# A new order for the pieces of two interleaved layers: where transposes, scores and roundings stand in each step's queue

## The chip, the cores and the metric

The kernel runs on one core of a Trainium2 chip. A core has a matrix engine (TensorE, "PE" in the profile, with its weight loads as "PEld"), a vector engine (VectorE, "DVE"), an activation engine (ScalarE, "ACT"), a general engine (GpSimd, "POOL") and a queue engine that issues transfers ("SP"). Each engine works through its own list of instructions in order; semaphores make one engine wait for another. The metric is the device time of one execution in microseconds (us).

## The reference

Eight layers are applied to `x` (16 batches x 128 tokens x 256 columns, float32), each as `x = x + tanh(gate) * layer(layernorm(x))`. Four are attention-like, four are feed-forward. The change touches mainly the part of the program in which three of them are computed together: the grouped-query attention of layer pair 1, its feed-forward layer with rounded weights and activations, and the decayed running sum of layer pair 2.

```python
# attention of pair 1: 16 query heads of 16 columns, 4 key heads, context as keys and values
Q = (query @ Wq).reshape(b, q_len, G, Hpg, dh) / math.sqrt(dh)
scores = einsum('bqghd,bkgd->bghqk', Q, K) + m * rel          # ALiBi slopes
out = einsum('bghqk,bkgd->bqghd', softmax(scores), V) @ Wo
# feed-forward of pair 1
def act_quant(x):
    scale = 127.0 / clip(max(abs(x), axis=-1, keepdims=True), EPS)
    return clip(round(x * scale), -128.0, 127.0) / scale
def weight_quant(w):
    scale = 1.0 / clip(mean(abs(w)), EPS)
    return clip(round(w * scale), -1.0, 1.0) / scale
bitlinear = lambda x, w: einsum('bsd,hd->bsh', act_quant(x), weight_quant(w))
y = bitlinear(silu(bitlinear(x, w1)) * bitlinear(x, w3), w2)   # 256 -> 704 -> 256
# layer of pair 2: r = decay * r + k*v along the tokens, out = q * r   (k = v = context)
```

## The kernel before

`stage_l1x` (from line 991) is the joint pipeline. Its main loop (line 1140) counts steps `n` from -4 to 22. In step `n` the attention of batch `n` is in the middle of its way: its scores and exponentials are made (`weigh`, two halves of two key heads each), while batch `n-1` is multiplied with its values (`mix`) and normalised, batch `n-2` is turned and projected (`turn_o`, `output`), and batch `n+4` gets the expert outputs of the layer before and its layernorm statistics (`collect`, `stats`). Queries are made for two batches at once, one half of the heads in an even step and the other half in an odd one.

`following` (line 1172) supplies the layers that follow. Here two batches, a pair `q`, go through together, over six steps. Batches `2q` and `2q+1` leave the attention in step `2q+3`; then come, in steps `2q+3` to `2q+8`: statistics (`stats`), normalisation and the largest magnitude (`normal`, `largest`), rounding (`rounded`), a transpose (`turn`), the two up-projections per batch with SiLU (`up`), rounding of the hidden row (`hidden`), its six transposes (`turn_hidden`), the down-projection (`down`), the squares and decayed sums of the context (`scanned`), and the layer of pair 2 (`retain_normal`, `retain`). The dictionary `order` (line 1413) says in which step after `2q+3` and at which of four places of that step a piece is issued; `then(m, place)` issues what stands there. A second list, `early` (line 1264), rounds the three weight matrices in steps 0 to 5: `total` sums magnitudes (VectorE), `size` adds them over the partitions (a small matmul), `rounded_weight` scales and rounds (ScalarE), `integers` clips (VectorE). From step 6 on the weights of the next stage are fetched by six transfers on POOL's queue.

For PE, VectorE and ScalarE the order of instructions is written out by hand (`manual_schedule`, line 996): each of these engines executes exactly in the order in which the Python code issues. POOL and SP are ordered by the compiler framework.

Two pools of PSUM hold what PE writes. `pss` has two buffers of two banks each (tag "s"): scores `s`, the up-projection `fu` and the hidden transposes `fh` go there in turn. `pst` has four buffers of one bank each (tag "a"), for everything else. PE can't write a buffer before its previous contents have been read. So for instance the scores of a step wait until ScalarE has copied `fh`, and the second half of an up-projection waits until VectorE has multiplied the first.

Names in the profile: `to` turn_o, `av` mix, `tx` turn_x, `tq` queries, `y` output, `ta` normalise, `fx` turn, `fh` turn_hidden, `fu` up, `fy` down, `fr` retain, `ts` size, `pt` the exponentials, `avs`, `oT`, `xT`, `qa` the copies out of PSUM.

Of the kernel before, what the change touches and what calls it, by code (L numbers as in the profile page):

```python
# [14 lines left out]
ALU = mybir.AluOpType  # L15
AX = mybir.AxisListType
# [39 lines left out]
def passage(ctx: ExitStack, tc: tile.TileContext, a: dict, out: bass.AP, inv, flag):  # L56
# [934 lines left out]
    def stage_l1x(wq, wo, ka, vbuf, collect, work, follow):  # L991


        with tc.tile_pool(name="l1", bufs=1) as l1, tc.tile_pool(name="l1w", bufs=2) as wk_, tc.tile_pool(
# [104 lines left out]
            def normalise(b):  # L1099
# [6 lines left out]
                sums_seen(0, rc.rearrange("p j g -> p (j g)"))  # L1106
                os_[b] = wk_.tile([P, 4, 4, 16], F32, name="o")
                nc.vector.tensor_tensor(os_[b].rearrange("p g j d -> p j g d"), t[:, :, :, 0:16], bc(rc, 3, 16), ALU.mult)

# [29 lines left out]
            begun, then = follow(pss, pst)  # L1139
            for n in range(-4, B + 7 + e):  # L1140
                p, odd = divmod(n, 2)
                fill()
                when(turn_o, n - e - 2)
                then(n - e, 0)
# [4 lines left out]
                when(mix, n - e - 1)  # L1149
                then(n - e, 1)  # L1150
                if search:
                    when(top, n, 1)
                if odd:
                    when(queries, p + 1, 1, n=B // 2)
                else:
                    when(turn_x, p + 1, n=B // 2)
                when(normal, n + 4)
                if n < 0:
                    fill()
                then(n - e, 2)  # L1160
                when(output, n - e - 2)
                when(weigh, n - e, 0)
                if not odd:
                    when(queries, p + 1, 0, n=B // 2)
                when(normalise, n - e - 1)
                when(weigh, n - e, 1)
                if n >= 0:
                    begun(n)
                then(n - e, 3)


    def following(sh, dcol):
# [6 lines left out]
        def follow(pss, pst):  # L1179
# [74 lines left out]
            def integers(i):  # L1254
# [10 lines left out]
                0: [layout],  # L1265
                1: [lambda: total(0), lambda: total(1)],
                2: [lambda: total(2), size, lambda: rounded_weight(0)],
                3: [lambda: integers(0), lambda: rounded_weight(1)],
                4: [lambda: integers(1), lambda: rounded_weight(2)],
                5: [lambda: integers(2)],  # L1270
            }

            def begun(n):
                if n == 0:
                    assert not work
                for f in early.get(n, ()):
                    f()
                if n == 6:
                    l2we.append(moe2_weights())
                if n >= 6 and l2we[0][1]:  # L1280
                    l2we[0][1].pop(0)()
# [56 lines left out]
            def up(q, i):  # L1338
# [21 lines left out]
                hm = v[f"hm{q % 2}"]  # L1360
                nc.vector.tensor_reduce(
# [68 lines left out]
            def then(m, place):  # L1430
                for (d, at), fs in order.items():
                    q, odd = divmod(m - 3 - d, 2)
                    if at == place and not odd and 0 <= q < B // 2:
                        for f in fs:
                            f(q)

            return begun, then

        return follow

# [624 lines left out]
```

## Time and profile before

| | |
|---|---|
| time before, median of 3 runs | 1077.6 us (1077.56 to 1077.85) |
| the profiled execution | 1077.04 us, span 1075.3 us |
| mean granted clock of PE | 0.904 |
| busy over the span: PE, DVE, ACT, POOL | 84%, 56%, 42%, 32% |
| joint pipeline, step 0 (first scores) to the last instruction of `retain` | 353.2 to 583.8 us |
| steps 0 to 15 (with scores) end | 537.3 us |
| 451.1 to 501.5 us, four full steps: PE, DVE, ACT busy | 43.8, 39.4, 34.1 of 50.4 us |

A line of the timeline gives the start, the busy time of the merged run of instructions, the engine, the line of the code, the operation, output and inputs, the number of instructions, and in brackets how long the engine had been idle and who ended that. A line of windows gives, for a stretch, its length and then the busy time of PE, PEld, DVE, ACT and POOL with the number of instructions, the share of the full clock that was granted to PE, and the load of the transfers. The granted clock is 1.00 or 0.50 at any moment.

### The profile page before, as it was taken

To read this page: it belongs to the slowest core of one execution; us is meant where nothing else is said; L and a number is where in the kernel's file an instruction comes from. 1 tells how busy PE (TensorE), PEld (TensorE's weight loads), DVE (VectorE), ACT (ScalarE), POOL (GpSimd) and SP (SyncE) were. 2 spreads that over 40 slices of the span, in tenths; PEclk is the share of its full clock that TensorE was granted. 3 is DMA by queue.
4 is the path that set the end of the run, shared out by engine and by line. 5 is a ranking of instruction groups with operands and counts; after the bars stand their busy time and mean duration, and the time that the engine had idled before them with its cause. 6 is when DMAs were issued, how large, how long until landed. Compare 5 with 4: busy or idle time off the path is not lost. (4 is left out here: it accounts for less than half of the span.)

```text
span 1075.3 us, 14892 instructions
## 1 busy us (share of the span) xinstructions
PE 904.1 (84%) x5212; PEld 602.5 (56%) x5212; DVE 607.5 (56%) x1537; ACT 456.8 (42%) x707; POOL 342.3 (32%) x389
## 2 busy tenths in 40 slices
PE   3899978899999888888864858998169999998797
PEld 1444456677778444455443747887145555555564
DVE  5988966322225656787788586454345555534442
ACT  1211024223322446666762242454257777882111
POOL 5766322543115324211111046550443342201000
PEclk9999979999999978999986557899579999997999
DMA  9100070233341109800000202352488887530000
GB/s 305 41 1 1 0 220 21 63 104 109 69 143 50 39 20 144 78 1 1 1 1 1 78 1 88 109 145 82 142 247 235 220 222 195 164 79 1 20 30 32
DMA packets 71401, 94.12 MB, mean 88 GB/s; under 512 B 9271, under 2 KB 63127, under 8 KB 69015
## 3 DMA queue, kind: packets, MB, share of 16 engines
q1 hardware_dynamic: 56952, 67.21, 21.1%
q0 software_dynamic: 14080, 23.78, 11.4%
q10 hardware_dynamic: 288, 2.10, 0.5%
q8 instruction: 45, 0.74, 0.3%
q14 instruction: 36, 0.29, 0.1%
HBM read 57.06 MB, written 33.55 MB: 84 GB/s over the span
## 5 line engine op out<-in xcount | busy, mean ns | idle before, releaser
L1667 ACT ACTIVATE pt<-s 128x1024 f32<-128x1024 f32 x128 | 126.4, 1024 | 32.5 <-PE s L1660 29.8
L709 POOL DMA_INDIRECT yc<-ys,pos x64 | 62.4, 975 | 125.0 <-DVE x L729 49.2
L297 PE MATMUL y<-kv,toep 128*128 128x512 f32 x192 | 86.6, 602 | 1.6 <-DVE toep L237 1.6
L1660 PE MATMUL s<-qa,ka 64*128 64x256 f32 x512 | 64.3, 332 | 8.3 <-ACT pt L1667 7.5
L1676 PE MATMUL av<-pt,v 128*32 128x256 f32 x1024 | 69.4, 389 | 0.1
L289 POOL TENSOR_TENSOR kv<-ctxT 128x1024 f32<-128x1024 f32 x32 | 60.2, 1900 | 28.3 <-PE y L297 28.3
L1660 PEld LDWEIGHTS s<-qa,ka 64*128 64x128 f32 x512 | 38.6, 188 | 46.9 <-issue 23.2
L1687 DVE COPY avs<-av 128x256 f32<-128x256 f32 x64 | 27.1, 423 | 65.5 <-PE av L1676 48.5
L297 PEld LDWEIGHTS y<-kv,toep 128*128 128x128 f32 x192 | 35.6, 192 | 43.7 <-issue 40.3
L616 PE MATMUL ub<-L0we,xbT 128*128 x160 | 50.8, 460 | 2.6 <-ACT xbT L607 2.6
L593 POOL DMA_INDIRECT xb<-xs,who x40 | 38.2, 954 | 43.3 <-PE tb L605 33.2
L913 PE MATMUL yb<-L2we,hT 88*128 (+1 forms) x224 | 41.7, 315 | 9.6 <-DVE hT L737 3.9
L848 POOL DMA_INDIRECT xb<-xs,who x40 | 38.1, 953 | 31.7 <-PE tb L860 20.9
L302 DVE TENSOR_TENSOR pr<-y,qT 128x1024 f32<-128x1024 f32 x32 | 39.0, 1222 | 12.1 <-PE y L297 9.4
L1567 POOL TENSOR_TENSOR hl<-f,hl 128x512 fp32r<-128x512 f32 x16 | 20.5, 1282 | 79.5 <-ACT hl L1566 79.5
L477 PE MATMUL up<-L0s,xT 128*128 128x352 f32 x128 | 43.0, 482 | 0.0
L913 PEld LDWEIGHTS yb<-L2we,hT 88*128 88x128 f32 x224 | 33.6, 205 | 16.5 <-DVE hT L737 9.0
L1086 PE MATMUL s<-qa,ka 18*128 18x512 f32 x128 | 37.4, 660 | 4.9 <-ACT follow L1380 4.9
L305 DVE TENSOR_REDUCE oT<-pr 128x128 f32<-128x1024 f32 x32 | 38.9, 1219 | 1.0
L1676 PEld LDWEIGHTS av<-pt,v 128*32 128x32 f32 x1024 | 26.9, 110 | 20.4 <-issue 0.7
L642 PE MATMUL yb<-L0we,hTb 88*128 x160 | 37.9, 379 | 0.0
L616 PEld LDWEIGHTS ub<-L0we,xbT 128*128 128x128 f32 x160 | 28.8, 190 | 15.5 <-ACT xbT L607 2.8
(384 smaller groups left out, 2043.1 us busy)
## 6 DMA issues: line engine op xcount, KB each, us to landing
scr<-hl SPq DMA_DIRECT2D x64, 256.0 KB
ys<-ysb SPq DMA_DIRECT2D x40, 256.0 KB
qa<-scr SPq DMA_DIRECT2D x32, 256.0 KB
ka<-scr SPq DMA_DIRECT2D x32, 256.0 KB
L2we<-in_L_w_dram POOLq DMA_DIRECT2D x6, 792.0 KB
L0we<-in_L_w_dram SPq DMA_DIRECT2D x6, 704.0 KB
xs<-xn SPq DMA_DIRECT2D x8, 512.0 KB
x<-in_x_dram SPq DMA_DIRECT2D x4, 512.0 KB
```

The source lines that it names most:

```text
L289: nc.gpsimd.tensor_tensor(t, bc(ch, 3, 8), bc(ch, 2, 8), ALU.mult)
L297: nc.tensor.matmul(y[:, ns], lhsT=T[:, h, d : d + P], rhs=kv[mc][:, ns], start=(mc == 0), stop=(mc == lc))
L302: nc.vector.tensor_tensor(pr, y.rearrange("p (b j i) -> p b j i", b=B, j=8), bc(qT[:, lc, :, hs], 2, 8), ALU.mult)
L305: nc.vector.tensor_reduce(oT[:, lc, :, hs], pr, AX.X, ALU.add)
L477: nc.tensor.matmul(t[:, n, 0 : 2 * I], lhsT=xT[:, c, b * P : (b + 1) * P], rhs=s13[:, c, n, :], start=(c == 0), stop=(c == 1),)
L593: nc.gpsimd.indirect_dma_start(out=xbs[s][:, i, :], out_offset=None, in_=xs, in_offset=bass.IndirectOffsetOnAxis(ap=who[:, 2 * s + i : 2 * ...
L616: nc.tensor.matmul(t[:, i, 0 : 2 * I], lhsT=xbT[:, i, c, :], rhs=we[:, bass.ds(regs[s][i] + c * 2 * I, 2 * I)], start=(c == 0), stop=(c == 1),
L709: nc.gpsimd.indirect_dma_start(out=got[b][:, i, :], out_offset=None, in_=ys, in_offset=bass.IndirectOffsetOnAxis(ap=pos[:, i, b : b + 1], ...
L913: nc.tensor.matmul(y[:, i, :], lhsT=hT[:, x, k, i, :], rhs=we[0:HI, bass.ds(at[i] + 4 * I + k * D, D)], start=(n == 0), stop=(n == 3),)
L1660: nc.tensor.matmul(s[:, h, jj, :], lhsT=ka[r, 2 * i + jj, sc * P : (sc + 1) * P], rhs=qa[r, 2 * i + jj, :], start=True, stop=True,)
L1667: nc.scalar.activation(pts[b, i][:, sc], s, AF.Exp)
L1676: nc.tensor.matmul(av[c : c + 32, :], lhsT=va[:, sc, 8 * h + 2 * i + jj, :], rhs=pt[:, sc, h, jj, :], start=(sc == 0), stop=(sc == 1),)
```

## The change

The pieces stay what they are; their order in the step changes. `then` now has five places (1 to 5) instead of four; `begun` is gone, and the weight rounding (`early`) is entered in the same numbering. Within one place, pieces of an older pair come first.

- `turn_hidden` of the two halves no longer follow one another. The first comes at the head of the even step, directly after `turn_o` and before `mix`; the second after the queries, between the two halves of the scores. `hidden` of the first half moves to the end of the odd step, that of the second half to after `turn_x`.
- The maximum over a hidden row (`largest_hidden`) is cut out of `up` and done for each half by itself, with its own limit, reciprocal, factor and POOL product.
- `up` of the first half moves behind `mix` and `down`, that of the second behind the queries. `down` moves from behind the queries to behind `mix`.
- At the end of the odd step `scanned` comes first, then `hidden`, then `stats`; before, `stats` came first.
- `rounded` moves from the head of the even step to behind the queries; `largest` and `normal` come later too; the statistics for pair 2's layer move behind the queries, `retain_normal` to the end of the step, and `fr` is issued before `fx`.
- The weight rounding is spread over other places of steps 1 to 5.
- In both attention layers the two VectorE instructions of `sums_seen`, which watch the range of the softmax sums, follow the product `o` instead of preceding it.

```diff
                 rc = small.tile([P, 4, 4], F32, name="rc")
                 nc.vector.reciprocal(rc, t[:, :, :, 16])
-                sums_seen(0, rc.rearrange("p j g -> p (j g)"))
                 os_[b] = wk_.tile([P, 4, 4, 16], F32, name="o")
                 nc.vector.tensor_tensor(os_[b].rearrange("p g j d -> p j g d"), t[:, :, :, 0:16], bc(rc, 3, 16), ALU.mult)
+                sums_seen(0, rc.rearrange("p j g -> p (j g)"))
...
             for n in range(-4, B + 7 + e):
                 p, odd = divmod(n, 2)
+                m = n - e
                 fill()
-                when(turn_o, n - e - 2)
-                then(n - e, 0)
+                when(turn_o, m - 2)
+                then(m, 1)
...
                 when(stats, n + 4)
-                when(mix, n - e - 1)
-                then(n - e, 1)
+                when(mix, m - 1)
+                then(m, 2)
...
                 if odd:
                     when(queries, p + 1, 1, n=B // 2)
                 else:
                     when(turn_x, p + 1, n=B // 2)
+                then(m, 3)
                 when(normal, n + 4)
                 if n < 0:
                     fill()
-                then(n - e, 2)
-                when(output, n - e - 2)
-                when(weigh, n - e, 0)
+                when(output, m - 2)
+                when(weigh, m, 0)
                 if not odd:
                     when(queries, p + 1, 0, n=B // 2)
-                when(normalise, n - e - 1)
-                when(weigh, n - e, 1)
-                if n >= 0:
-                    begun(n)
-                then(n - e, 3)
+                then(m, 4)
+                when(normalise, m - 1)
+                when(weigh, m, 1)
+                then(m, 5)
...
             early = {
-                0: [layout],
-                1: [lambda: total(0), lambda: total(1)],
-                2: [lambda: total(2), size, lambda: rounded_weight(0)],
-                3: [lambda: integers(0), lambda: rounded_weight(1)],
-                4: [lambda: integers(1), lambda: rounded_weight(2)],
-                5: [lambda: integers(2)],
+                (1, 5): [layout],
+                (2, 4): [lambda: total(0), lambda: total(1)],
+                (2, 5): [lambda: total(2)],
+                (3, 2): [size],
+                (3, 4): [lambda: rounded_weight(0)],
+                (3, 5): [lambda: rounded_weight(1)],
+                (4, 3): [lambda: integers(0)],
+                (4, 4): [lambda: integers(1)],
+                (4, 5): [lambda: rounded_weight(2)],
+                (5, 3): [lambda: integers(2)],
+                (6, 5): [lambda: l2we.append(moe2_weights())],
             }
...
-                hm = v[f"hm{q % 2}"]
-                nc.vector.tensor_reduce(
-                    hm[:, 0, i : i + 1], v[f"hid{i}"][:, 0:HID], AX.X, ALU.max, apply_absolute_value=True
-                )
-                if i == 1:
-                    nc.vector.tensor_scalar(hm[:, 0], hm[:, 0], Q_EPS, None, ALU.max)
-                    nc.vector.reciprocal(hm[:, 1], hm[:, 0])
-                    nc.vector.tensor_scalar(hm[:, 1], hm[:, 1], 127.0, None, ALU.mult)
-                    nc.gpsimd.tensor_scalar(hm[:, 2], hm[:, 0], v["s2t"], None, ALU.mult)
+
+            def largest_hidden(q, i):
+                hm = [v[f"hm{q % 2}"][:, n, i : i + 1] for n in range(3)]
+                nc.vector.tensor_reduce(hm[0], v[f"hid{i}"][:, 0:HID], AX.X, ALU.max, apply_absolute_value=True)
+                nc.vector.tensor_scalar(hm[0], hm[0], Q_EPS, None, ALU.max)
+                nc.vector.reciprocal(hm[1], hm[0])
+                nc.vector.tensor_scalar(hm[1], hm[1], 127.0, None, ALU.mult)
+                nc.gpsimd.tensor_scalar(hm[2], hm[0], v["s2t"], None, ALU.mult)
...
             order = {
-                (0, 3): [lambda q: stats(q, "f")],
-                (1, 0): [lambda q: normal(q, "f", [v["xn"][:, i, :] for i in range(2)]), largest],
-                (1, 1): [rounded],
-                (1, 3): [turn],
-                (2, 0): [lambda q: up(q, 0)],
-                (2, 1): [lambda q: up(q, 1)],
-                (3, 0): [lambda q: hidden(q, 0), lambda q: hidden(q, 1)],
-                (3, 1): [lambda q: turn_hidden(q, 0)],
-                (3, 2): [lambda q: turn_hidden(q, 1)],
+                (0, 5): [lambda q: stats(q, "f")],
+                (1, 1): [lambda q: normal(q, "f", [v["xn"][:, i, :] for i in range(2)])],
+                (1, 3): [largest],
+                (1, 4): [rounded],
+                (1, 5): [turn],
+                (2, 2): [lambda q: up(q, 0)],
+                (2, 3): [lambda q: largest_hidden(q, 0), lambda q: up(q, 1)],
+                (2, 5): [lambda q: hidden(q, 0)],
+                (3, 1): [lambda q: turn_hidden(q, 0), lambda q: largest_hidden(q, 1)],
+                (3, 3): [lambda q: hidden(q, 1)],
+                (3, 4): [lambda q: turn_hidden(q, 1)],
                 (4, 2): [down],
-                (4, 3): [scanned],
-                (5, 0): [lambda q: stats(q, "r")],
-                (5, 1): [retain_normal],
-                (5, 3): [retain],
+                (4, 5): [scanned],
+                (5, 4): [lambda q: stats(q, "r")],
+                (5, 5): [retain_normal, retain],
             }

             def then(m, place):
-                for (d, at), fs in order.items():
+                for f in early.get((m, place), ()):
+                    f()
+                if place == 5 and l2we and l2we[0][1]:
+                    l2we[0][1].pop(0)()
+                for (d, at), fs in sorted(order.items(), reverse=True):
                     q, odd = divmod(m - 3 - d, 2)
                     if at == place and not odd and 0 <= q < B // 2:
                         for f in fs:
                             f(q)
```

In `order`, the first number is the step counted from `2q+3` and the second the place. Even steps carry the entries with first number 1, 3 and 5, odd steps those with 0, 2 and 4. The same move of `sums_seen` is made in the attention of pair 3 (line 1700). The place of the step at which the six transfers of the next stage's weights are issued, one in each step from step 6 on, stays the end of the step.

## The prediction

> **What bounds the kernel now.** The chain of waits that ended last doesn't help: followed back from the end, it reaches only to 749 us, long after the joint pipeline. So I read the pipeline's own stretch. First the windows, from 426 us to its end (columns: length, then busy PE, PEld, DVE, ACT, POOL, and the granted clock):
>
> ```profile
> 451.10:476.50 25.40, 22.45 (x121) 12.71 (x120) 21.12 (x62) 17.00 (x26) 3.89 (x9) 0.93 0.02 6
> 476.50:501.50 25.00, 21.35 (x121) 12.46 (x120) 18.23 (x54) 17.11 (x26) 3.06 (x7) 1.00 0.00 1
> ...
> 537.30:583.80 46.50, 28.34 (x154) 18.65 (x152) 37.98 (x104) 23.88 (x39) 6.71 (x14) 0.80 0.00 1
> ```
>
> Two steps take 25 us and PE is close to full; in the tail without scores (46.5 us) VectorE is. The PE timeline shows what PE still waits for, here in the steps 11 to 13:
>
> ```profile
> 489.59 1.13 PE L1086 MATMUL s<-qa,ka 18*128 18x512 f32 x4
> ...
> 491.23 0.41 PE L1114 MATMUL to<-ident,o 128*128 128x128 f32 x2 [0.52 <-DVE o L1108]
> 491.69 1.97 PE L1095 MATMUL av<-pt,v 128*32 128x512 f32 x8
> ...
> 494.35 0.87 PE L1379 MATMUL fh<-ident,follow 128*128 128x128 f32 x6 [0.69 <-ACT follow L1372]
> ...
> 498.09 1.13 PE L1086 MATMUL s<-qa,ka 18*128 18x512 f32 x4 [0.91 <-ACT follow L1380]
> ...
> 504.34 0.47 PE L1344 MATMUL fu<-w1q,follow 128*128 128x352 bf16 x2 [0.46 <-ACT follow L1334]
> ...
> 507.73 0.46 PE L1344 MATMUL fu<-w1q,follow 128*128 128x352 bf16 x2 [1.03 <-DVE follow L1352]
> ```
>
> Start to start, scores cost 1.06 a half (489.00 less 487.94), `tq` 1.8, `y` 0.95, `av` 1.0, `ta` 0.56, `to` 0.34, `tx` 0.44, `fh` 0.71, `fx` 0.5, `fr` 0.43, one of four `fu` 0.6, `fy` 1.3. Over a pair (twice `to`, `av`, `ta`, `y`, `tq`, `fh`, four half scores) that is 20.1 of 25.0 us. So 4.9 us a pair are stalls, the most that any order can gain there: 0.58 before `to`, 0.95 inside `av`, 0.69, 0.91, 0.46, 1.03. ScalarE's timeline says why `av` and `fh` are late:
>
> ```profile
> 488.83 0.48 ACT L1049 ACTIVATE qa<-tq,consts 128x256 f32<-128x256 f32 x1 [4.12 <-DVE qa L1048]
> 489.32 1.28 ACT L1089 ACT_TABLE_LOAD   x1
> 490.62 1.94 ACT L1089 ACTIVATE pt<-s 128x1024 f32<-128x1024 f32 x2
> 492.44 0.72 ACT L1286 ACTIVATE ctxT<-ctxT 128x256 f32<-128x256 f32 x2
> ...
> 493.31 1.85 ACT L1372 ACTIVATE follow<-follow 128x704 f32<-128x704 f32 x2
> ```
>
> The query copy waits 4.1 us for VectorE's, which stands behind the work on `up`; the exponentials, squares and roundings queue behind it. Last, the clock:
>
> ```profile
> 425.61:429.02 3.41, 2.51 (x16) 1.35 (x15) 1.29 (x5) 2.22 (x4) 3.31 (x4) 1.00 1.14 209
> 429.02:432.43 3.41, 2.38 (x17) 0.95 (x17) 0.75 (x2) 2.73 (x5) 0.00 (x0) 1.00 2.25 234
> ...
> 463.15:466.57 3.42, 2.90 (x14) 1.04 (x14) 3.32 (x13) 2.68 (x4) 0.29 (x1) 1.00 0.00 0
> 466.57:469.98 3.41, 3.35 (x12) 0.86 (x12) 2.78 (x9) 3.41 (x7) 0.73 (x1) 0.50 0.00 0
> ...
> 521.18:524.59 3.41, 2.30 (x12) 1.02 (x12) 1.99 (x10) 2.88 (x4) 0.71 (x1) 1.00 0.02 5
> 524.59:528.01 3.42, 3.42 (x16) 2.43 (x13) 0.97 (x4) 1.95 (x3) 0.00 (x0) 0.50 0.00 0
> ```
>
> It changes on a grid of 3.41 us. The stretch before each fall (463.15, 521.18) held only scores of 18 rows, transposes and stalls. Leaving the scores out, matmuls and transposes filled 0.26 and 0.17 of it; the stretch at 425.6, with 0.43, was not followed by a fall. I take 0.4 as the line, and 1.7 us of PE work lost in a busy half-clock stretch.
>
> **The steady pair in the new order.** I walk the queues with these durations, the odd step from its `to` at t = 0. PE: `av` 0.34, `fy` 1.34, `fu` 2.65. ScalarE loads SiLU's table 0.87 after the first `fu` starts (505.21 less 504.34), so SiLU at 4.81, VectorE's product at 5.40, and the third `fu`, which needs that buffer, at 6.04. `tq` (1.8) now fills that gap, leaving 0.39 of the 1.03. VectorE goes on: second product 5.94, `qa` 6.50, the maximum with its three small instructions (1.4) 6.89, third product 8.29. The scores reuse its buffer: `y` ends at 8.19, scores start at 8.93, a new stall of 0.74; `ta` 9.99, second scores 10.58 to 11.64.
>
> The even step, from that end, z = 0. `to` starts at once (0.58 gained). `fh` now stands before `av` and needs the exponential (ends z = 1.1), two squares and `hidden`, all ScalarE: it starts at 2.65, a stall of 2.31 after `to`. Then `av` 3.36, `tx` 4.36, `y` 4.80, scores 5.75, `tq` 6.81, second `fh` 8.61, `ta` 9.32, scores 9.88 to 10.94. VectorE, held by the squares, starts the scan at 1.48, `stats` 2.67, maximum 3.95, `normal` 5.35, `collect` with statistics (1.78) 6.05, `largest` 7.8, then `normal` of batch n+4, `y`'s sum, and `qa` at 9.78. Where gathers stand before POOL's reciprocal root, that takes 2.46 from the variance (370.21 to 372.67) and `qa` is at 10.86. Without `collect` it waits only for `tq`: 8.85. ScalarE then has `qa` (+0.51), the copy of `fh`, and `rounded`, which starts 1.70 after VectorE's `qa`; `fx` follows, and the next odd step starts 1.53 after `rounded`. Adding the odd step's 11.64, a pair takes 24.65, with gathers 25.73, without `collect` 23.72. Before: 25.95, 25.46, 24.98, 24.97, 21.70 for the pairs ending in steps 7, 9, 11, 13, 15 (starts of `s`). After, at an unchanged clock: 25.7, 25.7, 24.7, 23.7, 21.7. That is only 1.6 less over all five: three stalls are exchanged for a long one.
>
> **The clock at that long stall.** From 8.19 in the odd step to z = 3.36 PE has 6.8 us with scores, `ta`, `to`, one `fh` and 3.05 of idling. Any grid stretch starting between t = 7.3 and 12.5 stays under 0.4, and 5.2 exceeds 3.41: every pair gets a half-clock stretch, half of them two. It falls on `fh`, `av`, `tx`, `y`, scores, and delays `tq` by 0.8 to 2.05, about 1.7. Where VectorE is late anyway that is hidden, so I add 0.3, 0.3, 1.0, 2.0 and 1.9 to the five pairs: 26.0, 26.0, 25.7, 25.7, 23.6, or 127.0 against 123.1. **+3.9**, between -1.6 (no more falls than now) and +6.5 (two everywhere: five times 2.05 on 121.5, less what VectorE hides in the first two).
>
> The Trainium skill, "TensorE: Matmul & The Clock Gate", section "PE-mode transpose", says that transposes don't count as activity for the gate. The trace here disagrees: 425.6, nearly only transposes and scores, kept the full clock. By the page, `fx`, `fr`, `ta` and `to` at the end of the even step would bring another fall per pair, and the sum would be about 5 us higher (an estimate from that page).
>
> **Steps 2 to 5.** Now PE waits 2.7 for `size` (from 373.7), then 2.39 for `xT` (390.2), and has half clock from 391.5 to 408.5; step 5's scores end at 414.3. In the new order `total` 0 and 1 delay `normalise` instead: `to` still starts at 376.5, and `size` adds 0.4. In step 4 `xT` no longer stands behind `rounded`, `tq` starts around 391.5, and the rest of step 4 is set by ScalarE's exponential, `rounded_weight` 2 (1.66) and `fx`'s copy: `fu` at 399.5 instead of 402.5, with one fall of the clock near 388. Step 5 then needs 9.0 plus 1.85 for `integers` 2 in front of the third product: 410.4 to 411.5. **-3.3**, between 0 (the 17 us at half clock stay) and -4.6 (no new fall).
>
> **The tail,** from the last scores' end: VectorE's queue gives 46.5, as now. The separate maxima cost it three small instructions (0.48) more a pair; `stats` before the wait for POOL's root (1.01 from the variance) is a hole that `largest` and `normal` don't fill. If `fy` and `fu` in steps 19 and 21 run at half clock, as 0.80 in that window says of now, they come 1.7 and 1.1 later than VectorE. **+1.7**, between 0 and +3.2.
>
> **At nothing:** `sums_seen` behind `o` in pair 3's attention: `o` ends at 853.5 and `tt` starts at 855.2; without that cover 32 times 0.17 is 5 us, a gain. The additional POOL product (0.3): nobody waits for it before `down`. `layout`'s 3.2 us on POOL ran at 340, beside the fills; later it could delay one root, +2. The six weight transfers keep one queue and were issued at 416, when `integers` ended; they are used after 660. SP's transfers don't move. VectorE's `qa` still goes before ScalarE's, now 1.2 instead of 4.1.
>
> **Sum:** 3.9 - 3.3 + 1.7 = +2.3 on the profiled 1077.04: 1079.3. The median lies 0.6 above the profiled run: 1079.9.
>
> **Rivals.**
> - *The clock falls no more often than now* (faster). For it: three boundaries of about ten fell, and the line at 0.4 comes from a few stretches. Then the pairs give -1.6, steps 2 to 5 -3.3, the tail 0: 1077.6 - 4.9 = 1072.7. It decides if the falls cost the five pairs less than about 3 us in all.
> - *Early gain lost and two falls at each boundary* (much slower): 0 + 6.5 + 3.2, 1087. For it: the stall stands at every pair, and step 4's stalls (1.1 in `av`, 0.75 before `y`) are such stretches too. Against: matmuls at half clock fill a stretch and bring the clock back.
> - *No effect:* stalls are exchanged and the sum is 0. Gains of 4.9 and losses of 5.5 would have to cancel: 1077.6.
>
> **How the numbers follow.** Forecast 0.45 (own range 1077.8 to 1083), faster rival 0.30 (1069 to 1075.4), much slower 0.18 (1083 to 1088), no effect 0.07. Of the forecast about 0.13 lies within 0.2% (2.2 us, what can be told from no change). So faster 0.30, same 0.20, slower 0.50. The range leaves out a tenth at each side: 1071 to 1086.
>
> **What would show it.** Right: `fh` with 2.3 us of idling after `hidden` in each even step, no wait of `to` for `o`, third `fu` waiting 0.4, scores of odd steps waiting 0.7 for VectorE's product; half-clock stretches near each such `fh`; `fu` first at about 399.5. Wrong: `fh` starting within 1.5 us of `to`, pairs under 24 us with `collect`, the clock full from 430 to 520, or POOL's order making VectorE wait elsewhere.

## The result, and the profile after

The changed kernel takes 1084.32 us (median of 15 runs, 1078.47 to 1091.17) against 1077.56 us (15 runs, 1073.46 to 1080.67) of the kernel before on the same chip: ratio 1.0064, 95% interval 1.0046 to 1.0082, so 5.0 to 8.8 us slower. The forecast was 1079.9 (1071 to 1086), slower with a chance of 0.50.

The profiled execution of the changed kernel took 1078.47 us (span 1076.7, mean granted clock 0.906). It was the quickest of its 15, so its total says little. I compare stages instead, cut at instructions that both kernels have: the *beginning* runs from the first scores to the start of the second scores of step 5, the *pairs* lie between the starts of the second scores of steps 5, 7, 9, 11, 13 and 15, and the *end* goes from there to the rounding of the gate's weights, behind the last `retain`.

| stage, us | before | after | difference |
|---|---|---|---|
| up to the first scores | 353.2 | 352.1 | -1.2 |
| beginning | 60.0 | 55.5 | -4.4 |
| pairs | 26.0, 25.5, 25.0, 25.0, 21.7 = 123.1 | 26.9, 25.8, 25.9, 26.6, 22.8 = 128.0 | +5.0 |
| end | 47.6 | 52.3 | +4.65 |
| behind the pipeline | 491.4 | 488.8 | -2.6 |
| sum | 1075.3 | 1076.7 | +1.4 |

The changed stages alone lost 5.2 us. The stages outside, whose work is the same, gave 3.8 back in this execution; part of that goes with the half-clock stretch that follows the pipeline, which reached 53.4 us behind the gate's rounding before and 51.3 us after.

The windows of after, for two pairs and for the part without scores (columns: length, then busy PE, PEld, DVE, ACT, POOL, the granted clock, transfers):

```profile
460.30:486.20 25.90, 22.85 (x121) 13.53 (x120) 20.28 (x62) 17.22 (x27) 3.95 (x9) 0.87 0.00 1
486.20:512.90 26.70, 23.64 (x123) 13.94 (x122) 16.63 (x50) 17.34 (x27) 2.84 (x7) 0.87 0.00 1
536.70:587.90 51.20, 30.81 (x154) 20.66 (x152) 40.08 (x115) 24.30 (x39) 7.35 (x17) 0.73 0.00 0
```

Against the windows of before, PE is busier (23.64 of 26.70, where it was 21.35 of 25.00) and at a lower clock: the same products took longer. The end has 0.73 of the clock where it had 0.80. The PE timeline of after, in steps 12 and 13, shows which stalls went and which came:

```profile
487.29 0.44 PE L1114 MATMUL to<-ident,o 128*128 128x128 f32 x2
489.95 1.54 PE L1373 MATMUL fh<-ident,follow 128*128 128x128 f32 x6 [2.22 <-ACT follow L1366]
491.42 1.94 PE L1095 MATMUL av<-pt,v 128*32 128x512 f32 x8
...
501.57 0.83 PE L1328 MATMUL fx<-ident,follow 128*128 128x128 f32 x4
...
508.45 0.46 PE L1339 MATMUL fu<-w1q,follow 128*128 128x352 bf16 x2 [0.30 <-DVE follow L1347]
...
511.20 1.13 PE L1086 MATMUL s<-qa,ka 18*128 18x512 f32 x4 [0.53 <-DVE follow L1347]
```

`to` no longer waits, the scores of the even step no longer wait for the copy of the second `fh` (0.91 before), and `fu` waits 0.30 instead of 1.03. In their place stands one stall of 2.22 us before `fh`, and 0.53 before the scores. Over the five pairs PE's waits come to the same sum, 16.8 us before and 16.7 after; what differs is the time at half clock in them, 10.2 us before and 30.2 after. ScalarE's timeline of after shows what `fh` waits for: the exponential, two squares, then the rounding of the hidden row.

```profile
487.41 1.02 ACT L1089 ACTIVATE pt<-s 128x1024 f32<-128x1024 f32 x1 [0.62 <-PE s L1086]
488.33 0.71 ACT L1281 ACTIVATE ctxT<-ctxT 128x256 f32<-128x256 f32 x2
488.94 0.96 ACT L1366 ACTIVATE follow<-follow 128x704 f32<-128x704 f32 x1
```

The windows of after on the clock's grid, around this stall and the next:

```profile
485.56:488.97 3.41, 2.17 (x12) 0.92 (x10) 1.23 (x6) 2.59 (x5) 0.00 (x0) 1.00 0.00 0
488.97:492.39 3.42, 2.44 (x14) 1.34 (x14) 3.25 (x10) 2.05 (x4) 0.74 (x2) 0.50 0.00 0
492.39:495.80 3.41, 3.41 (x16) 1.92 (x8) 2.08 (x8) 1.98 (x4) 1.08 (x4) 0.50 0.00 0
512.86:516.27 3.41, 1.48 (x7) 0.48 (x6) 1.74 (x6) 2.79 (x5) 0.00 (x0) 1.00 0.00 0
516.27:519.68 3.41, 3.11 (x14) 1.34 (x14) 3.20 (x12) 1.40 (x3) 1.02 (x2) 0.50 0.00 0
```

In the first stretch PE was busy for 2.17 us, but apart from the scores of 18 rows only with `ta` and `to`, about 1.0 of 3.41; half clock follows for two stretches, on `fh`, `av`, `tx` and `y`. Such falls begin at 407.0, 437.8, 461.7, 489.0 and 516.3: one at every pair.

### The profile page after: what moved, and what is told of

It is laid out like the page before. It is cut to its first block, busy times and chain, and to the rows that moved or that the text cites. A ratio compares the mean times of both kernels' runs of the same rounds, so it can differ in the third digit from the quotient of the medians.

```text
span 1076.7 us, 14928 instructions
## 1 busy us (share of the span) xinstructions
PE 899.4 (84%) x5212; PEld 599.6 (56%) x5212; DVE 609.0 (57%) x1561; ACT 456.8 (42%) x707; POOL 343.8 (32%) x397
## 5 line engine op out<-in xcount | busy, mean ns | idle before, releaser
L1666 ACT ACTIVATE pt<-s 128x1024 f32<-128x1024 f32 x128 | 126.5, 1023 | 32.2 <-PE s L1659 29.5
L1659 PEld LDWEIGHTS s<-qa,ka 64*128 64x128 f32 x512 | 39.0, 190 | 46.3 <-issue 23.6
L1686 DVE COPY avs<-av 128x256 f32<-128x256 f32 x64 | 27.1, 423 | 66.1 <-PE av L1675 48.4
L913 PEld LDWEIGHTS yb<-L2we,hT 88*128 88x128 f32 x224 | 33.0, 202 | 20.9 <-DVE hT L737 10.2
L1089 ACT ACTIVATE pt<-s 128x1024 f32<-128x1024 f32 x32 | 32.7, 1021 | 18.1 <-PE s L1086 18.0
L1675 PEld LDWEIGHTS av<-pt,v 128*32 128x32 f32 x1024 | 26.9, 110 | 20.5 <-issue 0.9
```

The source lines that it names most:

```text
L913: nc.tensor.matmul(y[:, i, :], lhsT=hT[:, x, k, i, :], rhs=we[0:HI, bass.ds(at[i] + 4 * I + k * D, D)], start=(n == 0), stop=(n == 3),)
L1659: nc.tensor.matmul(s[:, h, jj, :], lhsT=ka[r, 2 * i + jj, sc * P : (sc + 1) * P], rhs=qa[r, 2 * i + jj, :], start=True, stop=True,)
L1666: nc.scalar.activation(pts[b, i][:, sc], s, AF.Exp)
L1675: nc.tensor.matmul(av[c : c + 32, :], lhsT=va[:, sc, 8 * h + 2 * i + jj, :], rhs=pt[:, sc, h, jj, :], start=(sc == 0), stop=(sc == 1),)
```

## The experiments

On the different chips the kernel before takes between 1063.4 and 1078 us, so each run is compared by its ratio to the kernel before on its own chip, and by its stages. The beginning has values 2 us apart for the same code, as the clock's grid falls: the changed kernel and the runs that keep its beginning show 55.5 where the first fall comes 24 us behind the first scores, and 57.7 to 57.9 where one comes 6 to 7 us behind them already.

**The change once more.** No edit.

> The changed kernel once more, unaltered, for a second profile. Theory (clock): the stall of 2.2 us before the first hidden transpose of each even step brings stretches at half clock, so again one or two such stretches stand near it in each of the five pairs of steps 6 to 15, wherever the grid of 3.41 us lies; the five pairs take 126 to 130 us together, steps 2 to 5 end about 3 us earlier than in the kernel before, the tail is 2 to 4 us longer. The ratio to the kernel before is 1.004 to 1.008. Rival (elsewhere): the pipeline differs by only 4 us as in the first profile, and what the median has over that comes from other stages, whose time then differs between the two profiles by 3 us or more.

Measured: 1071.77 us, ratio 1.0080 (1.0060 to 1.0101). Beginning 57.7; pairs 27.1, 25.8, 26.1, 26.7, 22.8 = 128.4; end 52.2. Pairs and end repeat the first profile to 0.4 us on another chip; the loss is no matter of one execution. The stages outside the pipeline took 10.4 us less than in the first profile, but the kernel before took 13.7 us less on this chip too, and it was not profiled there; so what the rival says of the other stages stays open.

**Is it the clock? Work added at the stall.** Four products of full width, into columns of the `fh` buffer that nothing reads:

```diff
 def turn_hidden(q, i):
     t = pss.tile([P, 8, P], F32, name="fh", tag="s")
+    if i == 0:
+        for _ in range(4):
+            nc.tensor.matmul(t[:, 6:8, :].rearrange("p n s -> p (n s)"),
+                             lhsT=ident, rhs=l1o[:, 0, :], start=True, stop=True)
```

> The changed kernel with four more matmuls (128 rows, 256 columns, float32, about 0.46 us each, 1.8 us in all), whose results nobody reads, in front of the first hidden transpose of each even step. The stall itself stays, ScalarE's work is unchanged. Theory (clock): the stretch is now filled to over a half, the clock does not fall there, and the five pairs take about 121.5 us instead of 127; the time falls by 4 to 6 us below that of the changed kernel, ratio to the kernel before 0.999 to 1.003. Rival (the stall alone costs the time): the clock's fall is a bystander; the pairs stay at 127 us, and the time is that of the changed kernel or up to 2 us more, ratio 1.006 to 1.009.

Measured: 1066.97 us, ratio 1.0031 (1.0016 to 1.0047), and without the edit 1.0080 on the same chip. Pairs 26.5, 26.0, 24.5, 24.8, 22.6 = 124.5, between the theory's 121.5 and the rival's 127; the ratio is just above the theory's range. Half clock in steps 0 to 15 fell from 41.0 to 27.3 us. The windows of this run on the clock's grid, around the boundary into step 10, where the run without the edit had half clock from 462.6 on:

```profile
459.88:463.30 3.42, 3.42 (x18) 1.66 (x17) 1.72 (x7) 2.41 (x3) 0.00 (x0) 1.00 0.02 5
463.30:466.71 3.41, 2.91 (x20) 1.49 (x18) 2.83 (x8) 2.70 (x6) 0.31 (x1) 1.00 0.00 0
```

and the filler in its PE timeline:

```profile
462.58 1.89 PE L1374 MATMUL fh<-l1o,ident 128*128 128x256 f32 x8
464.97 0.88 PE L1378 MATMUL fh<-ident,follow 128*128 128x128 f32 x6 [0.50 <-ACT follow L1366]
```

More work, and the pairs are 4.0 us shorter. The stall itself is no shorter (1.89 of filler and 0.50 of waiting); only the clock stays up, and not everywhere: falls of 3.4 us are left at 436.0, 487.2 and 528.2. So the loss in the pairs, 5.0 us, is mostly the clock's.

**The first hidden rounding one place earlier.**

```diff
-    (2, 5): [lambda q: hidden(q, 0)],
+    (2, 4): [lambda q: hidden(q, 0)],
```

> The changed kernel with the rounding of the first hidden half one place earlier in the odd step: before the second exponential instead of after it and the squares. This removes what the stalled transposes wait for. Theory (stall plus clock): the first hidden transposes start within 0.5 us of turn_o in every even step, the clock keeps full there in most pairs, PE gains up to 2 us a pair, which the pairs with collect lose again to VectorE's queue: 25.7, 25.7, 24.7, 22.6, 20.7, together 119 us; ratio to the kernel before 0.997 to 1.001. Rival (VectorE's queue sets the even step anyway): the pairs shorten by less than 3 us in all, ratio 1.003 to 1.006.

Measured: 1070.95 us, ratio 1.0068 (1.0048 to 1.0089). Pairs 24.6, 27.9, 27.0, 22.6, 25.5 = 127.6. `fh` now starts directly behind `to`, and the next stall grows instead. One line each of PE, ScalarE and VectorE of this run, in step 8:

```profile
447.46 1.39 PE L1328 MATMUL fx<-ident,follow 128*128 128x128 f32 x4 [3.84 <-ACT follow L1320]
...
445.66 0.47 ACT L1049 ACTIVATE qa<-tq,consts 128x256 f32<-128x256 f32 x1 [4.15 <-DVE qa L1048]
...
444.43 0.41 DVE L1026 TENSOR_SCALAR xn<-x,mv,rs 128x256 f32<-128x256 f32 x1 [1.22 <-POOL rs L1017]
```

`fx` waits 3.84 us for the rounding of the next group, which stands behind the copies of the queries and of `fh`; the queries' copy waits 4.15 us for VectorE's half, which stands behind the gathers, the maximum and a `normal` that waits for POOL's root. The clock falls there instead (at 445.9 and 473.2). The stall before `fh` covered a VectorE queue that was late anyway. So this edit gains little, 0.8 us in the pairs: removing the first stall alone moves the fall. That is what the rival said; the ratio is a little over its range.

**`fh` behind the mix.** `turn_hidden` of the first tile goes behind `av`, whose 1.0 us of products then runs in the stall:

```diff
-    (3, 1): [lambda q: turn_hidden(q, 0), lambda q: largest_hidden(q, 1)],
+    (3, 1): [lambda q: largest_hidden(q, 1)],
+    (3, 2): [lambda q: turn_hidden(q, 0)],
```

> The changed kernel with the first hidden transposes behind mix instead of before it, as in the kernel before; the rest stays. Theory (stall plus clock): the product with the values runs inside the wait for the rounding, so 1.0 us less stall a pair, and as it counts as activity, fewer stretches at half clock; the five pairs take 122 to 125 us, ratio to the kernel before 1.000 to 1.004. Rival (stall alone, the clock falls as before): 1.0 us in each of the three last pairs, 124 us with the same number of falls, ratio 1.003 to 1.005.

Measured: 1066.23 us, ratio 1.0024 (1.0012 to 1.0036). Pairs 24.9, 27.4, 24.5, 23.5, 21.1 = 121.4, half clock in steps 0 to 15 23.9 us. The five pairs are shorter than the theory's 122 to 125 and than before the change (123.1): PE's waits in them sum to 12.7 us instead of 16.5, and half clock to 13.6 instead of 30.6. What is left of the loss is the end: 51.7.

**The kernel before, once more,** for its stages on the chip of the next three.

> The kernel before, unchanged, for a split of its time into stages beside the runs of this call. From its first profile: the five steady pairs 123.1 us together, the stage from the last scores of the pipeline to the gate's weights 47.6 us, the beginning up to the second scores of step 5 60.0 us, 31 us at half clock in the pipeline. If the changed kernel's loss lies where the two traces put it, these stages repeat within 1 us each; if they were a matter of one execution, they scatter by 3 us and more.

Measured: one run, 1076.3 us. Beginning 58.2, pairs 27.0, 25.5, 25.0, 25.0, 21.7 = 124.1, end 47.0, half clock in steps 0 to 15 23.9 us (30.7 in the first profile). Four pairs repeat within 0.05 and the end within 0.7; the beginning is 1.8 shorter and the first pair 1.1 longer, so a difference of 2 us there tells little.

**The old places at the end, first try.** The pieces of the last two groups go back to the places of before, and those of the group ahead of them (`fifth`) in part; from step 16 on the younger group comes first within a place.

```diff
+last = {
...
+    (2, 1): [lambda q: up(q, 0), lambda q: largest_hidden(q, 0)],
+    (2, 2): [lambda q: up(q, 1), lambda q: largest_hidden(q, 1)],
+    (3, 1): [lambda q: hidden(q, 0), lambda q: hidden(q, 1)],
+    (3, 2): [lambda q: turn_hidden(q, 0)],
+    (3, 3): [lambda q: turn_hidden(q, 1)],
...
+}
+fifth = {u: fs for u, fs in order.items() if u[0] < 3} | {
+    (3, 1): [lambda q: largest_hidden(q, 1), lambda q: hidden(q, 1)],
+    (3, 2): [lambda q: turn_hidden(q, 0)],
+    (3, 3): [lambda q: turn_hidden(q, 1)],
+} | {u: fs for u, fs in last.items() if u[0] > 3}
...
-    for (d, at), fs in sorted(order.items(), reverse=True):
+    for (d, at), fs, j in sorted(pieces, key=lambda u: u[0], reverse=m < 16):
```

> The changed kernel, with the pieces that run after the last scores (those of the last two pairs, and the hidden rows of the pair before them) at the places they had before; the steady pairs stay as changed. Theory, that the end is longer because the second tile's hidden rows are now rounded two places later, behind the next group's normalising, so that ScalarE's queue (rounding, copy, rounding, copy) stands between the hidden rows and the next group's fx: the end comes to 48 to 49 us from 52.2 (the three extra small VectorE instructions of each group, 0.6 us, stay), the pairs stay at 128 us, the whole is 3 to 4.5 us quicker than the changed kernel (ratio to before about 1.004). Rival, that the end is longer because it begins at another place of the clock's grid and meets half clock earlier: it stays over 51 us.

Measured: 1090.2 us, ratio 1.0113 (1.0090 to 1.0136); pairs 128.5, end 53.9. The expectation fell. Cutting the end at the first `fu` of the seventh group shows where: from the last scores to there 10.1 us before, 13.5 after, 16.4 here; from there on 37.5, 38.8 and 37.5. Two lines of VectorE's and PE's timelines of this run:

```profile
550.94 0.88 DVE L1358 TENSOR_REDUCE follow<-follow 128x1 f32<-128x704 f32 x1
...
553.46 1.54 PE L1373 MATMUL fh<-ident,follow 128*128 128x128 f32 x6 [5.20 <-ACT follow L1366]
```

With the younger group first, the maximum of the second hidden tile stood behind the seventh group's normalising and maximum, and PE idled for 5.20 us where the two orders meet. The last part is back at the 37.5 of before, so the order does set it; the joint was badly made. The cut is not quite like for like: `down` of the group ahead (`fy`, 1.31 us) stands before this `fu` in the changed kernel and behind it in the two others.

**The same, with `fh` behind the mix.** Both edits above together.

> The changed kernel with both repairs: the first tile's hidden rows turned behind the attention's mix, and the old places behind the last scores. If the two losses are separate and add up: pairs 121 to 122 us, end 48 to 49 us, beginning 55.5 to 57.7 us, so 1062 to 1063 us, ratio to before 0.9975 to 1.000. If the repaired pairs owe their time to a lucky phase of the clock, the pairs come back to 125 us and over and the ratio is 1.002 or more.

Measured: 1076.31 us, ratio 1.0004 (0.9984 to 1.0024). Pairs 24.7, 27.4, 24.5, 23.4, 21.1 = 121.1, on another chip and at another phase of the grid, so the gain there is not luck. The end is 54.0, by the same bad joint.

**The weights' preparation at its old places.**

```diff
-    (2, 5): [lambda: total(2)],  (3, 2): [size],  (3, 4): [lambda: rounded_weight(0)], ...
+    (2, 5): [lambda: total(2), size, lambda: rounded_weight(0)],
+    (3, 5): [lambda: integers(0), lambda: rounded_weight(1)], ...
```

> The changed kernel, with the preparation of the weights (layout, totals, rounding, integers) at the ends of steps 0 to 5 where it stood before, and all else as changed. Theory, that the quicker beginning comes from these places: the stretch from the first scores to the second scores of step 5 goes from 55.5 to 57.7 us back to 59 to 61 us, and the whole is 2 to 4 us slower than the changed kernel (ratio to before about 1.011). Rival, that it comes from the order of the pieces of the feed-forward part, which begin at step 3: the beginning stays under 58 us and the whole does not change.

Measured: 1083.01 us, ratio 1.0061 (1.0038 to 1.0084). The beginning is 54.1, shorter still than the changed kernel's 55.5, so the theory fell: the new places of the weights' preparation do not bring the gain and cost about 1.4 there, by one profile each. The ratio is the changed kernel's, as the rival had it. The pairs came to 132.4, the last alone 28.7, with 17 us at half clock in a row from 513.1. Why the clock stayed down so long in this execution stays open.

**The end mended.** The maximum comes directly behind its products, in step 15, and both hidden tiles are rounded together in step 16:

```diff
-fifth = {u: fs for u, fs in order.items() if u[0] < 3} | {
-    (3, 1): [lambda q: largest_hidden(q, 1), lambda q: hidden(q, 1)],
+fifth = {u: fs for u, fs in order.items() if u < (2, 5)} | {
+    (2, 4): [lambda q: largest_hidden(q, 1)],
+    (3, 1): [lambda q: hidden(q, 0), lambda q: hidden(q, 1)],
...
-    for (d, at), fs, j in sorted(pieces, key=lambda u: u[0], reverse=m < 16):
+    for (d, at), fs, j in sorted(pieces, key=lambda u: u[0], reverse=m < 17):
```

> The first try to put the end back left 5.2 us of idling on TensorE at the meeting of the two orders (the maximum of the second tile's hidden rows stood behind the next group's normalising); from the first up products of the seventh group to the gate's weights it took 37.5 us, as before the change, where the changed kernel takes 38.8. So of the changed kernel's 4.65 us more, 3.3 should lie between the last scores and those products, and 1.3 behind them. Here the maximum comes directly behind its products in step 15, and both hidden tiles are rounded together in step 16, as before the change; all earlier steps are as changed. Theory: the stretch from the last scores to the seventh group's up products comes to 10 to 11 us (13.5 now), the end as a whole to 47.6 to 49 us, the whole 3 to 4.5 us under the changed kernel (ratio to before about 1.003). Rival, that the groups that come before, being later, set it: over 51 us again.

Measured: 1067.68 us, ratio 1.0040 (1.0027 to 1.0053). Pairs 128.5, as changed; from the last scores to the seventh group's `fu` 10.6 us, the rest of the end 37.8, together 48.3. The expectation held: 3.9 of the 4.65 us are back. ScalarE's timelines show what the places changed. First after, behind the last exponential:

```profile
538.34 0.96 ACT L1366 ACTIVATE follow<-follow 128x704 f32<-128x704 f32 x1
...
540.93 0.90 ACT L1374 ACTIVATE follow<-fh,follow 128x768 bf16<-128x768 f32 x1 [1.37 <-PE fh L1373]
542.83 0.58 ACT L1097 COPY avs<-av 128x512 f32<-128x512 f32 x1 [1.00 <-PE av L1095]
543.31 0.97 ACT L1366 ACTIVATE follow<-follow 128x704 f32<-128x704 f32 x1
545.25 0.90 ACT L1374 ACTIVATE follow<-fh,follow 128x768 bf16<-128x768 f32 x1 [0.97 <-PE fh L1373]
546.05 1.08 ACT L1320 ACTIVATE follow<-follow 128x256 f32<-128x256 f32 x2
```

and the mended run:

```profile
540.24 1.84 ACT L1366 ACTIVATE follow<-follow 128x704 f32<-128x704 f32 x2
541.99 0.57 ACT L1097 COPY avs<-av 128x512 f32<-128x512 f32 x1
542.51 0.90 ACT L1374 ACTIVATE follow<-fh,follow 128x768 bf16<-128x768 f32 x1
545.29 1.09 ACT L1320 ACTIVATE follow<-follow 128x256 f32<-128x256 f32 x2 [1.88 <-DVE follow L1312]
```

In the changed kernel the next group's rounding (line 1320), which `fx` and `fu` need, stands behind two rounds of rounding, transposing and copying hidden rows, and each copy waits for PE. With both roundings ahead, only one copy of hidden rows stands in front of it, and it waits for VectorE's maximum. That queue is not all of the 3.3 us. 1.3 of them are `down`, which stands elsewhere. About 1.1 are the clock: the changed kernel has half clock from 536.8 to 543.6, on `fh`, `av` and `y`; in the filler run the same `fh` starts as late (3.7 us behind the start of the last scores), no half clock follows, and the stretch takes 12.3 us instead of 13.5. Cut at the `to` that stands ahead of `down` and `fu`, the changed end loses 2.1 us before it and 2.6 behind it, and the mended run wins back 1.6 and 2.3.

**Both repairs.** `fh` behind the mix, and the mended end.

> Both losses taken away: the first tile's hidden rows are turned behind the attention's mix, and the end is as in the run beside it. If they add: pairs 121.1 to 121.5, end 47.6 to 49, beginning 55.5 to 57.7, so 4 to 6 us quicker than the kernel before: ratio 0.994 to 0.997. If the losses replace one another, 1.000 or more.

Measured: 1060.59 us, ratio 0.9973 (0.9959 to 0.9988). Beginning 55.5, pairs 121.2, end 48.35. By their stages they add up, and this kernel is 0.3% quicker than the one before. The ratio just misses the expected 0.994 to 0.997; in the profiled execution the part behind the pipeline took 484.1 us, where the run beside it took 480.3.

**And a shorter queue in front of the queries.** The attention's `normal` of the batch four ahead goes behind VectorE's half of the queries, from step 0 on:

```diff
     then(m, 3)
-    when(normal, n + 4)
+    if n < 0:
+        when(normal, n + 4)
...
     then(m, 4)
+    if n >= 0:
+        when(normal, n + 4)
     when(normalise, m - 1)
```

> As the run beside it, and the attention's normalising of the batch four ahead stands behind the queries' bias on VectorE (in front of it now, where it waits for GpSimd's root: 1.22 us of waiting in step 8, and the queries' copy on ScalarE waits 4.2 us for VectorE's). Theory, that VectorE's queue in front of the queries sets the even step now: the wait of fx for the rounding (2.70 us) falls to 1.5 us or less, and the pairs with gathers get 1 to 2 us shorter each, 117 to 120 in all; ratio 0.991 to 0.995. Rival, that something else ends there as late (fh's second tile, whose maximum follows it on VectorE): pairs over 120.5 and no change beside the run without it.

Measured: 1052.89 us, ratio 0.9907 (0.9887 to 0.9927). Pairs 23.4, 24.2, 24.2, 23.3, 21.1 = 116.1, a little under the expected 117. PE and ScalarE of the run without this edit, in step 8:

```profile
445.68 0.33 PE L1328 MATMUL fx<-ident,follow 128*128 128x128 f32 x1 [2.70 <-ACT follow L1320]
...
443.88 0.47 ACT L1049 ACTIVATE qa<-tq,consts 128x256 f32<-128x256 f32 x1 [4.16 <-DVE qa L1048]
```

and with it:

```profile
443.58 0.33 PE L1331 MATMUL fx<-ident,follow 128*128 128x128 f32 x1 [1.05 <-ACT follow L1323]
...
441.77 0.47 ACT L1049 ACTIVATE qa<-tq,consts 128x256 f32<-128x256 f32 x1 [2.52 <-DVE qa L1048]
```

`fx` is 1.65 us earlier after its stall, and all five pairs together are 5.0 us shorter (the pair ending in step 9 alone 3.3); the rival fell. This is the quickest kernel of the study, about 10 us under the one before on its chip.

**The first group's rounding in front of the queries again.** To the changed kernel:

```diff
-    (1, 1): [lambda q: normal(q, "f", ...)],
-    (1, 3): [largest],
-    (1, 4): [rounded],
+    (1, 1): [lambda q: normal(q, "f", ...), lambda q: q or largest(q)],
+    (1, 2): [lambda q: q or rounded(q)],
+    (1, 3): [lambda q: q and largest(q)],
+    (1, 4): [lambda q: q and rounded(q)],
```

> The changed kernel, except that the first group's maximum and rounding (step 4) stand where they stood before the change: the maximum directly behind the group's normalising, the rounding behind the mix and so in front of ScalarE's copy of xT and of the queries. Theory, that the quicker beginning comes from the queries' copies going first: xT's copy waits about 2.5 us behind the rounding again, step 4 goes from 9.2 back to 12 to 13 us, the stretch from the first scores to the second scores of step 5 from 55.5 or 57.7 (two phases of the clock's grid were seen) to 58.5 to 61, and the steady pairs stay at 127 to 129. Rival, that the room comes from elsewhere (weights prepared in other places, or the clock's phase): step 4 stays under 10.5 us.

Measured: 1077.02 us, ratio 1.0118 (1.0095 to 1.0141). The beginning is 61.4 against 57.7 with the same first falls of the clock, but not where theory had put it: step 4 (second scores to second scores) stayed at 9.2, and step 5 went from 15.1 or 15.3 to 18.3. Before, the queries' products waited for `xT`, which stood behind a rounding that waited for VectorE. The ScalarE lines of before:

```profile
391.02 1.09 ACT L1325 ACTIVATE follow<-follow 128x256 f32<-128x256 f32 x2 [2.53 <-DVE follow L1317]
392.02 0.56 ACT L1035 COPY xT<-tx 128x512 f32<-128x512 f32 x1
```

and of this run, with the first wait of PE that follows:

```profile
390.75 1.09 ACT L1320 ACTIVATE follow<-follow 128x256 f32<-128x256 f32 x2
391.74 0.56 ACT L1035 COPY xT<-tx 128x512 f32<-128x512 f32 x1
...
399.29 0.44 PE L1114 MATMUL to<-ident,o 128*128 128x128 f32 x2 [2.79 <-DVE o L1107]
```

Here the maximum is early enough and the rounding waits for nothing; but VectorE's `o` is late, because the first `integers`, a `normal` that waits for POOL and the second `integers` stand ahead of it. Both halves of the old arrangement were needed for the old stall: with the old weight places and the new rounding place step 4 takes 8.4 us, with the new weight places and the old rounding place 9.2, with both old 13.1. So either move makes step 4 short, but with the weights' move alone 3.2 of the 3.7 us are lost in step 5. The lines point at the maximum rather than the rounding. In the run with the mended end, whose first falls stand at the same places, the same pieces stand ahead of `o`, and `to` waits 0.32; here the maximum stands ahead of the gathers' sums as well, and everything behind it on VectorE, and so `to`, comes 1.3 us later, counted from the scores of step 4. The rest goes with half clock, which falls at 399.8 in addition and from 410.0 covers both halves of step 5's scores instead of one. The run moves maximum and rounding together, so they are not told apart by it.

## Why the prediction was right, and where it was off

**Slower, by the mechanism given, and too small.** 1079.9 was forecast and 1084.3 came. That is inside the range and beyond the likeliest case's own range (1077.8 to 1083). The errors of the pairs (+1.1) and of the beginning (-1.1) cancel, by luck; in the stages the excess over the forecast, 5.2 for 2.3, is the end's. By its time it falls into the slower rival's, by its mechanism it does not: the early gain was kept, and single and double falls stand side by side.

**The steady pair: right.** The marks came as named: `to` without a wait, `fh` 2.22 late (2.31 forecast), the third `fu` 0.30 (0.39), the odd scores 0.53 (0.74), half clock at each such `fh`, double at two of the four falls between 430 and 520, triple at the one of 407. The pairs took 26.9, 25.8, 25.9, 26.6, 22.8 against 26.0, 26.0, 25.7, 25.7, 23.6: +5.0 for +3.9 (+3.9 against the second profile of the kernel before). The filler run shows that the clock is the cause of 4.0 of them, the run with `fh` behind the mix that it is enough to fill the stall with work that is there anyway. The walk's other finding, that "three stalls are exchanged for a long one" and VectorE's queue is as late, was shown by the earlier rounding (fall moved, 127.6) and by `normal`'s move (116.1).

**The faster rival** needed falls that cost under 3 us. The changed kernel doesn't meet that. The kernel with `fh` behind the mix comes near it, and its pairs take 121.4 us, where the walk at an unchanged clock gave 121.5; as it also waits 3.8 us less than the changed kernel, that the numbers meet is partly chance.

**Steps 2 to 5: the size roughly right.** -3.3 forecast, -4.4 between the two profiles, -2.7 against the second profile of the kernel before. `fu` came first at 397.7 (399.5 forecast). The gain is in step 4 (9.2 us for 13.1), where `xT` no longer stands behind a late rounding, as forecast. What the forecast didn't say is that either move alone does this; that the new place of the weights' pieces helps as well was not so: alone it cost 1.4. And part of what the move of maximum and rounding is worth lies in step 5, on VectorE.

**The end: the step that failed.** "VectorE's queue gives 46.5, as now", +1.7, at most +3.2. Measured +4.65 (+5.3 against the second profile of the kernel before). VectorE's queue was not what set it: ScalarE alternates with PE over the two hidden tiles of each of the last groups, and the next group's rounding queues behind that. With these pieces at their old places the end took 48.3 us, 3.9 of the 4.65 less. About 1.1 us is half clock right behind the last scores, on `fh`, `av` and `y`, which I had not priced; what I had priced, half clock on the later `fy` and `fu` and the three small VectorE instructions, was not separated. I walked the moved `hidden` and `turn_hidden` through the steady pair and not through the end, where no attention work fills ScalarE's waits.

**At nothing: right where it could be seen.** The attention of pair 3 took 182.08 us from its first scores to its last before and 182.02 after, so `sums_seen` behind `o` is worth nothing there. The POOL product and the layout were not tried by themselves.

**The median.** I added 0.6 for the distance of the profiled run to the median. After the change that distance was 5.8 us, and 1.3 us in the repeat. What the slower executions add could not be seen, since none of them was profiled; it stays open.

**Transposes and the clock: as the prediction had it.** The windows of after, with the end of the even step before the last pair:

```profile
499.22:502.63 3.41, 3.40 (x24) 2.07 (x24) 3.23 (x13) 3.07 (x6) 0.71 (x1) 1.00 0.00 0
502.63:506.04 3.41, 3.41 (x27) 2.06 (x28) 2.14 (x6) 1.62 (x5) 0.00 (x0) 1.00 0.00 0
```

The first held one half of the scores (1.1 us), the end of `fh`, `ta`, `fr`, `fx` and `to`, all transposes, and only in its last 0.1 us the start of `av`; the clock stayed. The stretch from 485.56 held scores as well and about 1.0 us of transposes, and the clock fell. What differs is the transposes and the idling, so here they count. "TensorE: Matmul & The Clock Gate" of the Trainium skill, section "PE-mode transpose", says that the full clock does not engage for transposes, which would not count as busy "the same way"; read as no activity at all, as in the prediction, these windows speak against it once more. Transposes alone were not tried.

The prediction's line at 0.4, read from three stretches, holds over all 14 profiles. Steps 0 to 15 have 603 stretches of the grid at full clock. Counting matmuls and transposes from start to start and leaving out the scores of 18 rows, none of the 500 filled to more than 0.44 was followed by half clock, and 73 of the 75 under 0.36 were; between the two both were seen. With the scores, stretches filled to 0.92 and 0.96 were followed by half clock too, so the scores count for little.

## What to carry to other kernels

A stall of 2 us on the matrix engine can cost twice: once as waiting, and again as half clock on the products behind it. When several short stalls are merged into one, look whether the stretch of the clock's grid that holds it still has work, and put independent products into it, as the mix here. Walk a moved piece through the end of the pipeline as well as through its middle: there the work that covered its waits is gone, and an order chosen for the middle need not be kept.

## What the runs showed of the hardware that was not expected

Adding 1.9 us of useless products per pair made the kernel quicker, by 0.5% (ratio 1.0031 where it was 1.0080): the granted clock stayed at 1.00 over two stretches of 3.41 us where it had been 0.50. And a single stretch with about 1.0 of 3.41 us filled, apart from the scores of 18 rows, was enough for the fall, though PE counts as busy for 2.17 of it.
